# A state-space layer on one core: the cross part's products, the norm pieces and the filling rounds in another order

## The chip, the core and the metric

The kernel runs on one core of a Trainium2 chip. A core has five engines with queues of their own: TensorE (PE, matrix products), VectorE (DVE), ScalarE (ACT), GpSimd (POOL) and SyncE (SP, which here only issues DMA transfers). The metric is the device time of one execution in microseconds. The kernel before took 2694.33 us, the median of three runs (2692.2 to 2698.51).

## The reference

The whole kernel is a decoder of twelve layers on x of 32 sequences by 128 tokens by 128 channels, all in fp32. Only the first layer, a state-space layer, matters here. Its reference, cut to what matters (h counts 32 heads of 8 channels, the state has 128 entries, a chunk has 64 tokens, so that each sequence has two chunks):

```python
zxbcdt = einsum('bld,kd->blk', layernorm(x), in_proj_w)
z, xBC, dt_raw = split(zxbcdt)                  # 256, 512, 32 columns
xBC = silu(sum(xp[:, k:k + L] * conv_w[:, k] for k in range(4)) + conv_b)
x_ssm, B, C = split(xBC)                        # 256, 128, 128
dt = 0.001 + 0.099 * sigmoid(dt_raw + dt_bias)
dA = -exp(A_log) * dt;  Acum = cumsum(dA within a chunk)
L[q, s] = exp(Acum[q] - Acum[s]) for s <= q, else 0
y  = (C B^T * L) (x_ssm * dt)                   # inside a chunk
y += exp(Acum) * C (state after the chunk before)   # the cross part
y  = norm(y + D * x_ssm, gated with silu(z)) out_proj, layernorm, added to x
```

What the kernel calls the *cross part* is the contribution of the first chunk of a sequence to the second one: a product of the scaled x of the first chunk with the C B^T block across the chunks, times a decay that is spread over the heads by another product.

## The kernel before

**Work.** The 32 sequences form eight groups (G) of four (J). A *round* n works on one sequence, i = n // 4 is its group and j = n % 4 its place in the group. Rounds run from n = -2 to 31 (the loop begins at L1138). A round lasts about 9 us and a group some 37 to 40 us.

**Parts of a round.** `first(n)` (L966) runs two rounds ahead: a set of small products that this text calls *p1* (decays and C B^T blocks), their copy to the tile `cbl` on ACT (128x320, and an exponential of 64 columns), and the transposes *p2* of the convolved x, whose copy feeds the scaled tiles `right`, `xd`, `xe` on POOL. `second(n)` (L998) makes the 128x512 products into the two "two" tiles one round ahead, `exponentials` takes them on ACT (two of 128x1024), `weighted(n, 0)` and `weighted(n, 1)` multiply them with C B^T on DVE. `third(n)` (L1017) is the round's own 64 products into "acc", followed by the cross part: four products into a "ps" tile, a copy of it to `cbl` on ACT (128x256), and a multiplication on DVE that writes the tile `offs`.

**Parts of a group.** These are generators, of which `go` runs one step at a time: `entry` (L923; layer norm: statistics on DVE, a power on POOL, the four ACT activations to `xn` as its third step, the transposes to `xnT` as the fourth, and four ACT activations of the residual x as the fifth), `conv` (L862; four 128-channel blocks c = 0 to 3; for c = 2 the four taps are four products on PE, the `taps` products, for the others an ACT scaling and three multiply-adds on DVE follow the projection, then a tanh on ACT and a final multiplication on DVE), `gate` (L892; projection, copy to z, tanh on ACT, a multiplication on DVE), `decays` (L936; the product for dt, which DVE reads first into the tile `dts`, a tanh, small DVE operations, a second small product and an exponential), `joined` (L1040; sums the parts, gates, projects out, normalizes, adds to x).

**What sets the order.** PE, ACT and DVE keep the order in which the program is written: the class `Ordered` chains each instruction of an engine to the one before it, and `follow(T, A, V)` at L1097 switches that on for the layer. POOL is kept in order only in the prologue (L1098 to L1137); in the rounds a scheduler orders it. The DMA issues of SP are in program order. The PSUM tiles named "ps" have two buffers for everything (`ps()`, L220), so a product into a "ps" tile waits for the copy out of the tile two "ps" tiles earlier.

**Prologue and end.** The head of the kernel (from L284) issues the loads; `weights()` prepares the weights in two pieces; `fill()` clears and fills the kept tiles on POOL; `make_taps()` multiplies the taps of block 2 into the projection; then a list of `go` calls prepares group 0 and part of group 1 (L1100 to L1136). In the last rounds the next layer's generator `lead` (L1313) is run a step at a time: `prepare(0, 0)` loads a context tile and normalizes group 0's x (`normed`, L395, with its four scalings on POOL into `xn`), `prepare(0, 1)` transposes these on PE, then projections, and so on. In the kernel before, its steps run at the ends of rounds 27 to 31, and twice behind the loop.

Of the kernel before, what the change touches and what calls it, by code (L numbers as in the profile page):

```python
# [23 lines left out]
G = 8  # L24
J = 4
# [180 lines left out]
def program(ctx, tc, cols, x, ctxt, mask, drop, dfirst, dsmall, dwide, drows, dunits, dexperts, dconst, drel, dwq, out):  # L206
    nc = tc.nc
    V, A, T = (Ordered(tc, engine) for engine in (nc.vector, nc.scalar, nc.tensor))
    P, SY = Ordered(tc, nc.gpsimd), nc.sync
# [10 lines left out]
    def ps(shape=(128, 512), dtype=F32):  # L220
        return pp.tile(list(shape), dtype, tag="ps", name="ps", bufs=2)
# [14 lines left out]
    def gmid(shape=(128, 512), dtype=F32):  # L236
        return mid.tile(list(shape), dtype, tag="gmid", name="gmid", bufs=10)
# [41 lines left out]
    K = {n: cconst.view(cs, n) for n in cconst.at if cconst.at[n][1] < cconst.kept}  # L279
    ident = K["ident"]  # L280
# [2 lines left out]
    xg = []  # L283
    for i in range(G):  # L284
        t = const.tile([128, J, D], F32, name=f"x{i}")
        SY.dma_start(out=t, in_=x[i * J : i * J + J].rearrange("b s d -> s b d"))
        xg.append(t)
        if i == 0:
            SY.dma_start(out=ident, in_=dconst[:, 0:128])
            SY.dma_start(out=cs[:, 128:], in_=dconst[:, 128 : cconst.kept])  # L290
            w0 = units.tile([128, cfirst.n], F32, tag="unit", name="w0")
            A.dma_start(out=w0, in_=dfirst)
            ww = const.tile([128, cwide.n], F32, name="ww")
            A.dma_start(out=ww[:, 0 : cwide.early], in_=dwide[:, 0 : cwide.early].to_broadcast([128, cwide.early]))
# [6 lines left out]
    W0 = {n: cfirst.view(w0, n) for n in cfirst.at}  # L301
# [13 lines left out]
    onesb = const.tile([128, 128], BF16, name="onesb")  # L315
    V.memset(onesb, 1.0)
    identb = const.tile([128, 128], BF16, name="identb")
    V.tensor_copy(identb, ident)

    pick16 = const.tile([128, 4], BF16, name="pick16")  # L320
    V.tensor_copy(pick16, K["pick16"])
    flip = const.tile([128, 128], BF16, name="flip")
    V.tensor_copy(flip, W0["flip"])
    ctxT = [const.tile([128, 512], F32, name=f"ctxT{i}") for i in range(G)]


# [489 lines left out]
    def layer0(lead):  # L816
# [3 lines left out]
        def weights():  # L820

            A.activation(na, WW["m_A_log"], AF.Exp)
            V.tensor_scalar(na, na, -1.0, None, ALU.mult)
            yield
            for b in range(2):
                mean, block = small(1), W0["out"][:, b * 128 : b * 128 + 128]
                V.tensor_scalar(block, block, W0["norm_w"][:, b : b + 1], None, ALU.mult)
                V.tensor_reduce(mean, block, AX.X, ALU.add)
                V.tensor_scalar(mean, mean, -1.0 / 128, None, ALU.mult)
                V.tensor_scalar(block, block, mean[:, 0:1], None, ALU.add)  # L830
            V.tensor_scalar(W0["D"], W0["D"], 0.25, None, ALU.mult)
            yield

        block2 = W0["xbc"][:, 256:384]
# [2 lines left out]
        def make_taps():  # L837

            d, p = bmid((128, 4, 128)), ps((128, 4, 128))
            V.tensor_tensor(d, bc(ident, 1, 4), bc(W0["cw"][:, 8:12], 2, 128), ALU.mult)  # L840
            mm(flat(p), block2, flat(d))
            A.copy(taps[:, 0:512], flat(p))

        kept = [gbig((128, 2, 1024)) for _ in range(3)]
# [1 line left out]
        sides = [kept[0][:, n].rearrange("p (j s r c) -> p j s r c", j=J, s=2, r=4) for n in range(2)]  # L846

        def fill():
            for t in (*kept[0:2], more):
                P.memset(t, 0.0)  # L850
            for t in sides:
                for token, side, at in ((0, 0, 0), (64, 0, 8), (0, 1, 16)):
                    one = bc(bc(ident[:, token : token + 1], 1, J), 2, 4)
                    P.tensor_copy(t[:, :, side, :, at : at + 8], one.to_broadcast([128, J, 4, 8]))

        xds = [t.rearrange("p (a n m e) -> p a n m e", a=8, n=4, m=4) for t in (kept[1][:, 0], kept[1][:, 1], more[:, 0:1024])]
        rights = [kept[2][:, n, 0:512].rearrange("p (a k) -> p a k", a=8) for n in range(2)]
# [159 lines left out]
        def third(n):  # L1017

            i, j = n // J, n % J
            (xd, xe, cbl, _), m = fronts.pop(n), mids.pop(n)[0].rearrange("p s h q -> p (s h) q")  # L1020
            if j == 0:
                sums[i] = [acc((128, 2, J, 64)) for _ in range(2)]
                offs[i] = gmid((128, 2, J, 64))
            for b in range(2):
                for k in range(4):
                    for r in range(4):
                        for ch in range(2):
                            rows = slice(64 * ch, 64 * ch + 64)
                            mm(sums[i][ch][32 * r : 32 * r + 32, b, j], flat(xd[rows, 4 * b + r, k]), m[rows, 16 * b + 4 * r + k],
                               k == 0, k == 3)  # L1030
            p = ps((128, 2, 2, 64))
            for b in range(2):
                mm(p[:, 0, b], xe[:, 128 * b : 128 * b + 128], cbl[0:64, 64:128])
            for b in range(2):
                mm(p[:, 1, b], K["spread"][:, 128 * b : 128 * b + 128], cbl[:, 320:384])
            A.copy(cbl[:, 128:384], p.rearrange("p s b q -> p (s b q)"))
            both = cbl[:, 128:384].rearrange("p (s b q) -> p s b q", s=2, b=2)
            V.tensor_tensor(offs[i][:, :, j], both[:, 0], both[:, 1], ALU.mult)
# [50 lines left out]
        def go(what, g, *more):  # L1089

            if 0 <= g < G:
                key = what, g, *more
                if key not in late:
                    late[key] = what(g, *more)
                next(late[key], None)
# [6 lines left out]
        go(entry, 0)  # L1102
        go(entry, 0)
        fill()
        make_taps()
        go(entry, 0)
        next(prepared)
        go(conv, 0, 2)
        go(decays, 0)
        go(conv, 0, 3)  # L1110
        go(conv, 0, 2)
        go(entry, 1)
        go(conv, 0, 3)
        go(decays, 0)
        go(conv, 0, 2)
        go(conv, 0, 3)
        go(conv, 0, 0)
        go(decays, 0)
        go(entry, 1)
        go(conv, 0, 3)  # L1120
        go(conv, 0, 0)
        go(conv, 0, 1)
        go(decays, 0)
        go(conv, 0, 3)
        go(entry, 1)
        go(conv, 0, 0)
        go(conv, 0, 1)
        go(conv, 0, 0)
        go(conv, 0, 1)
        go(entry, 1)  # L1130
        go(conv, 0, 0)
        go(decays, 0)
        go(conv, 0, 1)
        go(conv, 0, 1)
        next(prepared)
# [2 lines left out]
        for n in range(-2, G * J):  # L1138
            i, j = n // J, n % J

            convs_now = [(1, 2)] if n == -2 else [(1, 3), (1, 0)] if n == -1 else [(i + 1, 1) if j == 0 else (i + 2, (2, 3, 0)[j - 1])]

            def go_conv():
                for g, c in convs_now:
                    go(conv, g, c)

            front = first(n + 2) if n + 2 < G * J else iter(())
            next(front, None)
            go_conv()
            next(front, None)  # L1150
            go_conv()
            if j == 0:
                go(decays, i + 1)
                go(gate, i, 0)
                go(joined, i - 2)
            elif j == 1:
                go(joined, i - 1)
            elif j == 2:
                go(decays, i + 2)
                go(decays, i + 2)  # L1160
                go(entry, i + 3)
                go(joined, i - 1)
            elif j == 3:
                go(gate, i + 1, 1)
                go(entry, i + 3)
                go(joined, i - 1)
            if 0 <= n + 1 < G * J:
                second(n + 1)
            go_conv()
            if 0 <= n + 1 < G * J:  # L1170
                exponentials(n + 1)
            if j == 1:
                go(joined, i - 1)
            elif j == 3:
                go(entry, i + 3)
            if 0 <= n + 1 < G * J:
                weighted(n + 1, 0)
            if 0 <= n < G * J:
                third(n)
            if 0 <= n + 1 < G * J:  # L1180
                weighted(n + 1, 1)
            if j == 0:
                go(entry, i + 2)
                go_conv()
            elif j == 1:
                go(entry, i + 2)
            elif j == 2:
                go(decays, i + 2)
                go(gate, i + 1, 1)
                go_conv()  # L1190
            elif j == 3:
                go(joined, i)
                go(gate, i + 1, 0)
                go_conv()
                go(decays, i + 2)
            go_conv()
            if n == -1:
                go(entry, 1)
            if n >= G * J - 5:
                next(lead)  # L1200
        next(lead)
        go(joined, G - 1)
# [1311 lines left out]
```

## Time and profile before

| | |
|---|---|
| median of three runs | 2694.33 us (2692.2 to 2698.51) |
| profiled execution | 2692.69 us, span 2690.9 us |
| mean granted clock of PE | 0.946 |
| state-space layer | 0 to about 365 us of the span |
| busy from 45 to 345 us (300 us) | PE 270.12, DVE 247.63, ACT 195.11, POOL 154.55 us |
| granted clock of PE there | 0.91 |
| busy from 0 to 45 us (prologue) | PE 26.55, DVE 22.87, ACT 18.88, POOL 14.14 us |

All times are microseconds from the start of the span. A line of the list in order of time has the start, the duration, the engine, the line of the helper that recorded it (L194 for nearly all, so that the tiles tell instructions apart), the operation, the tiles written and read with their shapes, how many instructions are merged (x4), and in brackets the idle time of the engine just before, with what ended it. A tile's buffer number is left out. A line of the waits has the engine that waited and its tile, after the arrow the engine and tile that ended the wait, then the total, the number and the longest. A line of the windows has the stretch, its length, the busy time of PE, of PE's weight loads, DVE, ACT and POOL (with their instructions), the granted clock of PE (1.00 is full speed, 0.50 half), the DMA engines' share and GB/s. The chain that ended last is told in pieces of start, duration, engine and tile.

### The profile page before, as it was taken

To read this page: it belongs to the slowest core of one execution; us is meant where nothing else is said; L and a number is where in the kernel's file an instruction comes from. 1 tells how busy PE (TensorE), PEld (TensorE's weight loads), DVE (VectorE), ACT (ScalarE), POOL (GpSimd) and SP (SyncE) were. 2 spreads that over 40 slices of the span, in tenths; PEclk is the share of its full clock that TensorE was granted. 3 is DMA by queue.
4 is the path that set the end of the run, shared out by engine and by line. 5 is a ranking of instruction groups with operands and counts; after the bars stand their busy time and mean duration, and the time that the engine had idled before them with its cause. 6 is when DMAs were issued, how large, how long until landed. Compare 5 with 4: busy or idle time off the path is not lost.

```text
span 2690.9 us, 59184 instructions
## 1 busy us (share of the span) xinstructions
PE 2387.5 (89%) x24663; PEld 1527.2 (57%) x24663; DVE 1983.8 (74%) x3972; ACT 1347.3 (50%) x2999; POOL 927.1 (34%) x979
## 2 busy tenths in 40 slices
PE   6999889999989999999998999988888987887755
PEld 3665567777744435556764444446665886544434
DVE  6888778888888756777776555569996338898993
ACT  5766544444422223344443445468983334665653
POOL 3454532322310214345651101144443444332432
PEclk8999899999999999999998999999998998998886
DMA  3000000000000010000000000000003463100000
GB/s 113 3 2 14 10 21 5 9 5 4 18 12 1 0 36 3 3 14 14 12 3 17 1 0 1 1 1 2 2 2 129 147 214 130 62 16 16 28 12 20
DMA packets 51966, 74.23 MB, mean 28 GB/s; under 512 B 4017, under 2 KB 42450, under 8 KB 51570
## 3 DMA queue, kind: packets, MB, share of 16 engines
q1 hardware_dynamic: 48786, 64.10, 7.5%
q0 software_dynamic: 2624, 5.40, 0.6%
q8 instruction: 194, 3.18, 0.5%
q10 hardware_dynamic: 288, 0.95, 0.1%
q14 instruction: 74, 0.61, 0.1%
HBM read 57.54 MB, written 12.89 MB: 26 GB/s over the span
## 4 chain that ended last, share of the span: by engine, by line
PE 56%; DVE 22%; ACT 6%; issue 2%; POOL 2%; DMA 0%; DVEq 0%; ACTq 0%; POOLq 0%
PE two L194 20%; PE ps L194 18%; PE acc L194 17%; DVE bbig L194 9%; DVE s L194 7%; ACT bbig L194 3%; DVE bmid L194 3%; POOL xn L194 1%; DVE x L194 1%; ACT bmid L194 1%; DVE gmid L194 1%; POOL s L194 1%; DVE h L194 0%; ACT L194 0%; ACT gmid L194 0%
## 5 line engine op out<-in xcount | busy, mean ns | idle before, releaser
L194 PE MATMUL two<-xnT,u 128*128 128x512 f32 x512 | 261.7, 612 | 9.3 <-ACT bmid L194 5.6
L194 DVE TENSOR_REDUCE s<-two 128x8 f32<-128x1024 f32 (+1 forms) x192 | 228.8, 1219 | 47.6 <-PE two L194 43.0
L194 DVE TENSOR_TENSOR bbig<-bbig 128x1024 f32<-128x1024 f32 (+3 forms) x232 | 248.2, 1111 | 14.3 <-ACT bbig L194 12.0
L194 PE MATMUL acc<-bmid,u 128*128 128x512 f32 x416 | 215.0, 603 | 13.4 <-DVE bmid L194 12.4
L194 PE MATMUL ps<-cs,bbig 128*128 128x128 f32 x1184 | 176.5, 289 | 47.6 <-ACT bbig L194 21.3
L194 DVE TENSOR_TENSOR bmid<-bmid,ps 128x512 f32<-128x512 f32 x192 | 129.9, 684 | 93.1 <-ACT bmid L194 71.0
L194 PEld LDWEIGHTS ps<-cs,bbig 128*128 128x128 f32 x1184 | 135.1, 146 | 101.2 <-ACT bbig L194 36.5
L194 PE MATMUL two<-gbig,gmid 32*128 32x512 f32 (+1 forms) x1248 | 186.3, 551 | 4.4 <-issue 2.1
L194 POOL TENSOR_TENSOR s<-s,nhalf 128x4 f32<-128x4 f32 x104 | 128.7, 1237 | 135.1 <-DVE s L194 116.5
L194 PEld LDWEIGHTS two<-xnT,u 128*128 128x128 f32 x512 | 91.4, 191 | 115.7 <-issue 56.6
L194 ACT ACTIVATE bbig<-two 128x1024 f32<-128x1024 f32 x96 | 94.8, 1025 | 116.7 <-PE acc L194 101.7
L194 DVE RECIPROCAL s<-acc 128x128 f32<-128x128 f32 x96 | 91.3, 951 | 83.6 <-PE acc L194 83.4
L194 ACT COPY bbig<-ps 128x512 f32<-128x512 f32 x166 | 91.4, 585 | 116.4 <-PE ps L194 116.3
L194 POOL TENSOR_TENSOR x<-x,ww 128x512 f32<-128x512 f32 x64 | 91.6, 1431 | 163.1 <-ACT xn L194 80.3
L194 ACT ACTIVATE bmid<-two,ws 128x512 f32<-128x512 f32 x128 | 85.2, 686 | 111.6 <-PE two L194 111.4
L194 POOL TENSOR_TENSOR bbig<-bbig,s 128x1024 f32<-128x1024 f32 x32 | 61.7, 1927 | 222.6 <-PE two L194 152.5
L194 ACT ACTIVATE bmid<-two 128x512 f32<-128x512 f32 x88 | 52.5, 597 | 164.0 <-PE two L194 159.2
L194 PEld LDWEIGHTS acc<-bmid,u 128*128 128x128 f32 x416 | 75.0, 192 | 101.0 <-issue 46.1
L194 ACT ACTIVATE bbig<-two,s 128x256 f32<-128x256 f32 x256 | 118.1, 477 | 25.4 <-DVE s L194 25.3
L194 ACT ACTIVATE bbig<-bbig,s 128x128 f32<-128x128 f32 x384 | 118.8, 390 | 6.8 <-DVE s L194 6.8
L194 POOL TENSOR_SCALAR gbig<-bmid,cs 128x512 f32<-128x512 f32 x64 | 99.2, 1566 | 49.0 <-ACT bmid L194 49.0
L194 PE MATMUL two<-xT,we 128*128 128x128 f32 (+1 forms) x576 | 100.4, 330 | 15.9 <-ACT xT L194 9.8
(331 smaller groups left out, 6267.0 us busy)
## 6 DMA issues: line engine op xcount, KB each, us to landing
we<-in_experts SPq DMA_DIRECT2D x36, 768.0 KB, 4.6
u<-in_units SPq DMA_DIRECT2D x10, 768.0 KB, 4.3
gmid<-in_ctx SPq DMA_DIRECT2D x16, 256.0 KB, 3.0
x<-in_x SPq DMA_DIRECT2D x8, 256.0 KB, 5.6
gmid<-in_mask SPq DMA_DIRECT2D x8, 256.0 KB, 3.1
ys<-bbig SPq DMA_DIRECT2D x2, 1024.0 KB, 6.2
gmid<-ys SPq DMA_DIRECT2D x8, 256.0 KB, 3.1
gmid<-in_drop SPq DMA_DIRECT2D x8, 256.0 KB, 3.5
```

The lines of the kernel that those rows point to most:

```text
L194: d = self.made = f(*args, **kwargs)
```

## The change

The work and the number of instructions stay the same. Seven things move:

1. the identity's load is issued ahead of the first tile of x on SP;
2. three casts on DVE (identb, pick16, flip) move from the head to the second piece of `weights()`;
3. `fill()` writes the sides right after the first memset, and clears the two other tiles behind them;
4. the cross part leaves `third(n)`, where it stood behind the round's sums and between the two weighted multiplications, and becomes `cross(n)`, called at the top of round n, ahead of `first(n + 2)`;
5. the list of `go` calls in the prologue has another order;
6. in rounds with j = 3, the step of `entry(i + 3)` with the four activations to xn moves from ahead of the weighted multiplication to behind the gate's copy and tanh;
7. the lead of the next layer runs at rounds 26, 28, 29, 30 and 31 instead of 27 to 31, so that its first step is one round earlier.

```diff
@@ the head
+        if i == 0:
+            SY.dma_start(out=ident, in_=dconst[:, 0:128])
         SY.dma_start(out=t, in_=x[i * J : i * J + J].rearrange("b s d -> s b d"))
         xg.append(t)
         if i == 0:
-            SY.dma_start(out=ident, in_=dconst[:, 0:128])
...
-    V.tensor_copy(identb, ident)
-    V.tensor_copy(pick16, K["pick16"])
-    V.tensor_copy(flip, W0["flip"])
@@ weights(), second piece
             V.tensor_scalar(W0["D"], W0["D"], 0.25, None, ALU.mult)
+            V.tensor_copy(identb, ident)
+            V.tensor_copy(pick16, K["pick16"])
+            V.tensor_copy(flip, W0["flip"])
             yield
@@ fill()
-            for t in (*kept[0:2], more):
-                P.memset(t, 0.0)
+            P.memset(kept[0], 0.0)
             for t in sides:
...
+            for t in (kept[1], more):
+                P.memset(t, 0.0)
@@ third(n)
-            (xd, xe, cbl, _), m = fronts.pop(n), mids.pop(n)[0].rearrange("p s h q -> p (s h) q")
+            xd, m = fronts.pop(n)[0], mids.pop(n)[0].rearrange("p s h q -> p (s h) q")
             if j == 0:
                 sums[i] = [acc((128, 2, J, 64)) for _ in range(2)]
-                offs[i] = gmid((128, 2, J, 64))
...
+        def cross(n):
+
+            i, j = n // J, n % J
+            _, xe, cbl, _ = fronts[n]
+            if j == 0:
+                offs[i] = gmid((128, 2, J, 64))
             p = ps((128, 2, 2, 64))
             for b in range(2):
                 mm(p[:, 0, b], xe[:, 128 * b : 128 * b + 128], cbl[0:64, 64:128])
@@ the prologue
         go(entry, 0)
         go(entry, 0)
         fill()
+        go(entry, 0)
+        go(conv, 0, 3)
+        go(decays, 0)
         make_taps()
-        go(entry, 0)
+        go(conv, 0, 3)
+        go(decays, 0)
+        go(entry, 1)
+        go(conv, 0, 3)
         next(prepared)
+        go(decays, 0)
+        go(conv, 0, 0)
         go(conv, 0, 2)
         go(decays, 0)
         go(conv, 0, 3)
+        go(conv, 0, 0)
         go(conv, 0, 2)
         go(entry, 1)
...
@@ the rounds
+            if 0 <= n:
+                cross(n)
             front = first(n + 2) if n + 2 < G * J else iter(())
...
             if j == 1:
                 go(joined, i - 1)
-            elif j == 3:
-                go(entry, i + 3)
             if 0 <= n + 1 < G * J:
                 weighted(n + 1, 0)
...
             elif j == 3:
                 go(joined, i)
                 go(gate, i + 1, 0)
+                go(entry, i + 3)
                 go_conv()
                 go(decays, i + 2)
...
-            if n >= G * J - 5:
+            if n >= G * J - 6 and n != G * J - 5:
                 next(lead)
```

More of the change, by code (lines that the diff above doesn't have):

```diff
@@ L1113, in layer0 @@
         go(conv, 0, 3)
-        go(decays, 0)
         go(conv, 0, 2)
-        go(conv, 0, 3)
+        go(conv, 0, 1)
+        go(conv, 0, 0)
+        go(entry, 1)
+        go(conv, 0, 1)
         go(conv, 0, 0)
@@ L1119, in layer0 @@
         go(entry, 1)
[L1120 to L1126, printed above, removed]
         go(conv, 0, 1)
         go(conv, 0, 0)
[L1129 to L1132, printed above, removed]
         go(conv, 0, 1)
```

## The prediction

> **What bounds the kernel now.** I read the waits of VectorE (DVE) and TensorE (PE) between 45 and 345 us of the span first, because the change touches only the state-space layer, which ends near 365 us; then the instructions in order of time around one round boundary, around the lead-in of the next layer and at the layer's end; last the busy time and granted clock of short windows.
>
> Waits of DVE, then of PE, 45 to 345 us (who waits, for whom: total us, times, longest):
>
> ```profile
> DVE bbig L194 <- ACT bbig L194: 16.3, 8, 8.0
> DVE gmid L194 <- ACT bmid L194: 11.6, 5, 5.3
> DVE dts L194 <- PE ps L194: 8.4, 6, 2.2
> DVE gmid L194 <- ACT cbl L194: 7.8, 13, 1.0
> PE ps L194 <- ACT cbl L194: 13.0, 20, 1.3
> PE ps L194 <- POOL xn L194: 6.1, 4, 3.6
> ```
>
> The reader is to see two things. DVE waits 8.4 us for the decay product (dts), six times, once in each group that still prepares a later one. So a group is a loop of two stretches: one that DVE fills, from dts to the end of convolution 1's three multiply-adds (148.03 to 173.33, 25.3 us), and a chain over PE and ScalarE (ACT) back to the next dts (136.63 to 148.03, 11.4 us). What lengthens the chain is paid each time. The row of 7.8 us is the wait that the change goes after: offs behind the cross part's copy.
>
> The chain in order of time (start, duration, engine, operation, idle before):
>
> ```profile
> 134.51 0.39 ACT L194 COPY cbl<-ps 128x256 f32<-128x256 f32 x1
> 134.76 0.62 ACT L194 COPY xnT<-ps 128x512 f32<-128x512 f32 x1
> 136.03 3.66 PE L194 MATMUL ps<-xnT,taps 128*128 128x512 f32 x8
> 136.72 0.63 ACT L194 ACTIVATE bmid<-gmid 128x512 f32<-128x512 f32 x1 [1.34 <-DVE gmid L194]
> ...
> 141.10 1.94 ACT L194 ACTIVATE bbig<-two 128x1024 f32<-128x1024 f32 x2
> ...
> 143.95 0.39 ACT L194 COPY cbl<-ps 128x256 f32<-128x256 f32 x1
> 144.20 1.67 ACT L194 ACTIVATE x<-x,s 128x128 f32<-128x128 f32 x4
> 145.75 0.43 ACT L194 COPY cbl<-ps 128x320 f32<-128x320 f32 x1
> ...
> 148.03 0.29 DVE L194 TENSOR_TENSOR dts<-ps,ww 128x128 f32<-128x128 f32 x1 [1.12 <-PE ps L194]
> ```
>
> The taps product (convolution 2) starts while ACT still waits 1.34 us for DVE with its tanh of convolution 1. The cross copy (128x256) stands ahead of that tanh at 134.51, and ahead of the residual's four activations at 143.95.
>
> **The change, part by part.** No instruction is added or removed; every cost is one of order. The sum is against the profiled execution (2692.69 us, span 2690.9), which lies 1.64 us under the median of the runs.
>
> *Cross part, j=1.* With two buffers for all "ps" tiles, each product waits for the copy out of the tile two earlier. Today the sequence is cross, xnT, p1, taps; then it is xnT, cross, p1, taps. So taps needs the cross copy, and in ACT's new order that copy stands behind the tanh that waits for DVE. New start of taps: the tanh's end, 0.39 for the copy, 0.07 to PE. At 136.72 that is 137.8 instead of 136.03, +1.77; at 98.27 it is +1.83; at 213.08, 173.53 and 252.03 it is +1.62, +0.97, +0.97, but there PE is at half clock until a fixed moment, so half of it comes back (0.81, 0.49, 0.49); at 64.99 ACT does not wait for DVE, +0.1. Sum +5.5; the bounds are 0 (all absorbed) and 7.3 (nothing comes back). Behind taps on PE stand p2, second and the exponentials' input, so DVE's weighted waits in its turn.
>
> *Cross part, j=2.* The cross copy now stands behind the four activations of x (1.67). Convolution 3's buffer is the cross's, so its product, its copy and the decay product follow in a row. From the exponentials' start: exponentials 1.81 and squares 1.04 to the next start, x 1.55, cross copy 0.43, product 1.12, bmid copy 0.66, decay product 1.19 to dts: 7.8, against 6.93 now (141.10 to 148.03). +0.87, six groups: +5.2. Bounds: 0, and 2.06 a group (all of 1.67 and 0.39), 12.4.
>
> *Offs behind the weighted pair.* The wait leaves the middle of the DVE stretch. Most of the 7.8 us becomes a wait at weighted or at dts instead, since those come from PE; in the stretch that DVE itself bounds I find 0.16 to 0.36 per group: -1.5. Bounds 0 and -7.8.
>
> *Norm pieces (xn, four activations, 1.65) behind the gate's copy and tanh, j=3.* PE gets the gate's tile back 1.65 us sooner (its waits for z are 4.4 us in all), but the next group's dts exponential, the cross copy and p1 come 1.5 to 1.85 later. I take 0: ACT has 2.5 us of wait for DVE in that round (at 131.24 it waits 2.49), which covers it; without that cover +1.85 per group, 11.1, and the best case is the z wait back, -4.4.
>
> *Clock.* Busy time in windows of the trace, ending with the clock granted:
>
> ```profile
> 134.11:137.52 3.41, 2.56 (x14) 1.72 (x15) 3.34 (x4) 2.07 (x5) 0.42 (x1) 1.00 0.00 0
> 168.24:171.65 3.41, 2.19 (x62) 1.77 (x43) 3.38 (x7) 3.41 (x7) 2.35 (x2) 1.00 0.02 5
> 171.66:178.48 6.82, 6.82 (x16) 3.83 (x17) 6.75 (x9) 1.49 (x4) 2.32 (x2) 0.50 0.00 0
> 209.20:212.61 3.41, 2.24 (x18) 1.93 (x17) 3.34 (x6) 3.09 (x5) 2.23 (x2) 1.00 0.03 5
> 212.62:216.02 3.40, 3.40 (x10) 1.70 (x9) 3.37 (x5) 1.07 (x3) 1.31 (x2) 0.50 0.00 0
> ```
>
> Second column: PE busy. After 2.56 us of 3.41 the clock stays at 1.00, after 2.19 and 2.24 the next window is granted 0.50, and taps takes 6.10 (173.53) instead of 3.66. The change takes 1.8 us out of the 2.56 of the first window. I charge the two groups at full clock now (98 and 136) about 2 us each: +4, nearer to the throttled rows than to none. Bounds 0, and six times 2.44 = 14.6.
>
> The Trainium skill ("TensorE: Matmul & The Clock Gate", "What's actually happening" and "HAM oscillation — how this bites in real kernels") says that the array falls to half rate after an idle window of about 3.4 us and comes back after a busy one. The longest idle time of PE ahead of 171.66 is 1.03 us, so the trace throttles earlier than the rule as worded. By the rule this term is 0 and the sum below 4 us lower; the rows decide.
>
> *Lead of the next layer one round earlier.* PE waits for POOL's norm with all its later work queued behind (PE is kept in order), then ACT and DVE:
>
> ```profile
> 323.59 6.06 POOL L194 TENSOR_SCALAR xn<-x,s 128x128 f32<-128x128 f32 x4
> 325.74 0.48 PE L194 MATMUL ps<-cs,xn 128*128 128x128 f32 x1 [3.57 <-POOL xn L194]
> 328.15 0.48 PE L194 MATMUL ps<-cs,xn 128*128 128x128 f32 x1 [1.94 <-POOL xn L194]
> 335.57 1.23 DVE L194 SCALAR_TENSOR_TENSOR bbig<-bbig,cbl 128x1024 f32<-128x1024 f32 x1 [7.97 <-ACT bbig L194]
> ```
>
> With xn ready, the transposes end near 322.8, and p1 (1.06), p2, second and the first exponential follow at their full-clock rows: weighted near 328.1 instead of 335.57, -7.4. The context load (256 KB, 3.0 us) on SP's queue moves with it; nothing of this layer stands behind it on that queue, so no cost. On POOL the norm (0.58, 1.25, 6.06) passes ahead of right(29), which makes second(29) about 1.8 late on PE; DVE is behind there, so I charge 0.4. Sum -7.0; bounds -9 (the half clock at 325 to 335 goes too) and +1.8 (right(29)'s delay paid in full, no gain).
>
> *End of the layer.*
>
> ```profile
> 353.71 2.10 PE ps L194 x8
> 355.90 0.38 ACT cbl L194
> 356.31 2.53 DVE gmid L194 x7
> ```
>
> This is the chain that ended last: the cross part lies between the last sum and the join. At the top of the round it is out of the way: 2.6 from 353.71 to 356.31. What is late next is the 16 "two" products (3.79) that stand behind it on PE and only move by 2.1, into DVE's reduces: I take -1.6, bounds -2.6 and 0.
>
> *Prologue.* The identity ahead of x0 on SP and two casts (0.23, 0.22) out of DVE's head remove its wait of 1.51; xnT (15.25) comes about 2.3 us earlier, and the cold taps product (6.42) no longer stands ahead of the decays (DVE idles 6.92 there). But taps must run later on the same PE, the weights' second part ends near 40 us in both, and x0's four loads land behind one more transfer: -1.0, bounds -3 and +0.5. Fill's other order and the casts lie beside idle time (POOL, 8.57 us of wait). Offs in rounds 26 to 30 outside the lead: -0.4 (waits of 0.63, 0.64, 0.73, mostly passed on); bounds -2 and 0.
>
> Sum: 5.5 + 5.2 - 1.5 + 4.0 - 7.0 - 1.6 - 1.0 - 0.4 = +3.2, so 2695.9 against the profiled execution and 2697.5 against the median; I say 2698. 0.2% is 5.4 us, about what a measurement of this kernel can tell from no change.
>
> **Rivals.**
> A (the sum): 2698, its own range 2692 to 2705.
> B, the clock decides: every group loses one taps pass to half clock. Six times 2.44 instead of 4.0 is +10.6: 2708. For it: windows at 2.56 busy lose 0.9 to 1.8. Against: the groups at 173, 213 and 252 us are throttled already, and a taps pass that is at half clock cannot lose the same 2.44 again.
> C, faster: the delays of j=1 and j=2 do not reach dts, because DVE arrives there later than the product. Then 5.5, 5.2 and 4.0 fall away, and 2698 - 14.7 = 2683. It decides if DVE comes over 1.1 to 1.3 us later to dts relative to PE than now (its waits at 110.26 to 266.47); the weighted pair, which moves with the exponentials, could do that. Against it: those waits exist in all six groups, so DVE is early today.
> D, the lead does not gain: POOL is late with right(29) and PE waits for that instead of xn. +7.0: 2705.
>
> **How the numbers follow.** Chances: A 0.46, B 0.22, C 0.24, D 0.08. A lies mostly within 0.2% (2688.9 to 2699.7): of it 0.27 same, 0.16 slower, 0.03 faster. B and D are slower, C faster. So faster 0.27, same 0.27, slower 0.46. The range 2684 to 2711 leaves out the better half of C and the worse third of B; A's neighbours and the bounds of the clock term fill the rest.
>
> **What would show it.** Right: the taps rows at 136.03 and 98.27 start about 1.1 us after convolution 1's last multiply-add ends; the cross copy stands behind the tanh; the wait of dts for PE grows from 8.4 to some 20 us; the offs wait vanishes from the DVE list; the 7.97 wait and the four waits for xn are gone; the join follows the last sum directly. Wrong: if dts waits no longer than now (C), if PE's mean clock from 45 to 345 us falls well below 0.91 (B), or if second(29) waits for POOL by over 3 us (D). Most likely to fail are the two chain terms, since they assume that nothing else shifts beside them.

## The result, and the profile after

The changed kernel takes 2714.74 us, the median of seven runs (2706.46 to 2723.93), against 2695.59 us for the kernel before on the same chips (seven runs, 2691.57 to 2698.51): a ratio of 1.0075, 95% interval 1.0057 to 1.0093. It is slower by 20 us, not by 4: outside the stated range of 2684 to 2711, on the side of rival B.

The profiled execution took 2716.11 us with a span of 2714.3 us. Three marks place the loss inside the layer: the first and the last dts row of the rounds on VectorE (DVE), and the first instruction of the join that ends the layer.

| | before | after | difference |
|---|---|---|---|
| first dts of the rounds | 42.0 | 41.0 | -1.0 |
| last dts (six groups later) | 266.5 | 288.4 | |
| the six groups between them | 224.5 | 247.4 | +22.9 |
| from the last dts to the join | 90.1 | 86.2 | -3.9 |
| join | 356.5 | 374.6 | +18.0 |
| from the join to the end of the execution | 2336.2 | 2341.6 | +5.4 |

The last row is scatter: the work behind the join is the same, and it took 2334 to 2346 us in the executions profiled here. So the six groups lose 23 us and the tail gains 4. The 1.0 us at the first dts says nothing yet: in the two other profiles with the prologue of before (the runs with the lead alone, below) the first dts came at 39.2 and 42.1, in those with the changed prologue between 39.9 and 42.1.

The stretch from 45 to 345 us, by busy time in the views of windows, here of after (columns: length, busy PE, PE's weight loads, DVE, ACT, POOL, then PE's granted clock):

```profile
45.00:345.00 300.00, 269.29 (x4727) 177.97 (x4726) 233.43 (x440) 184.87 (x363) 134.37 (x143) 0.84 0.02 6
```

Before, the clock there was 0.91 and PE was busy 270.12 us over 5220 matmul records; now it is busy as long for 4727 records. Since the clock is granted at 1.00 or 0.50 in all these traces, a mean of 0.91 is some 54 us at half clock in these 300 us (2 x 0.09 x 300), and 0.84 some 96 us.

The waits of DVE, PE and ScalarE (ACT) there, of after:

```profile
DVE dts L194 <- PE ps L194: 14.5, 5, 3.5
...
DVE gmid L194 <- ACT cbl L194: 6.4, 6, 1.2
...
PE ps L194 <- ACT cbl L194: 11.1, 7, 3.7
PE ps L194 <- ACT dts L194: 10.0, 6, 2.1
...
ACT bmid L194 <- DVE gmid L194: 5.3, 3, 2.5
```

DVE waits for dts 14.5 us instead of 8.4. The wait for offs has not gone: it is 6 waits, 6.4 us in all, instead of 13 and 7.8. New is the row in which PE waits for ACT's dts, 10.0 us (1.2 before). And ACT's wait for DVE ahead of its tanh and its copies is down to 5.3 us; the same row of before reads

```profile
ACT bmid L194 <- DVE gmid L194: 21.1, 11, 2.6
```

In the list in order of time, of after, one group shows two waits of PE:

```profile
129.95 1.64 ACT L194 ACTIVATE xn<-x,s 128x128 f32<-128x128 f32 x4
...
132.01 0.25 ACT L194 ACTIVATE dts<-ps 64x128 f32<-64x128 f32 x1
132.17 0.35 ACT L194 COPY cbl<-ps 128x256 f32<-128x256 f32 x1
...
132.31 0.71 PE L194 MATMUL ps<-w,gbig 128*128 128x64 f32 x4 [1.57 <-ACT dts L194]
...
141.43 3.66 PE L194 MATMUL ps<-xnT,taps 128*128 128x512 f32 x8
...
149.34 1.65 ACT L194 ACTIVATE x<-x,s 128x128 f32<-128x128 f32 x4
...
150.88 0.69 ACT L194 COPY cbl<-ps 128x256 f32<-128x256 f32 x2
...
151.30 1.13 PE L194 MATMUL ps<-xnT,w 128*128 128x512 f32 x2 [1.40 <-ACT cbl L194]
```

(The copy x2 at 150.88 is the cross copy and the 128x320 copy behind it, merged.) At j=3 the four xn activations now stand ahead of the decays' exponential, and p1, at the top of the next round, waits 1.57 us for it. At j=2 the cross copy stands behind the x activations, and convolution 3 waits 1.40 us. Each returns five times in the layer, at 1.57 to 1.58 and at 1.40 us. What follows two of them is in the windows, of after:

```profile
105.75:109.15 3.40, 2.00 (x19) 1.73 (x18) 2.15 (x3) 3.40 (x9) 1.89 (x2) 1.00 0.00 0
109.17:115.98 6.81, 6.56 (x24) 5.02 (x25) 3.30 (x13) 2.13 (x6) 4.12 (x6) 0.50 0.02 4
129.64:133.04 3.40, 1.83 (x14) 1.62 (x14) 3.40 (x7) 2.88 (x8) 0.00 (x0) 1.00 0.01 2
133.06:136.46 3.40, 3.40 (x14) 1.74 (x16) 3.37 (x11) 1.35 (x5) 2.22 (x1) 0.50 0.00 0
```

The wait of 1.40 us leaves a window with 2.00 us of work, the wait of 1.57 one with 1.83; the clock then is 0.50 for 6.81 and 3.40 us. Of the ten waits, nine have half clock that begins between 1.1 us before and 2.3 us after their end; behind the one that ends at 242.92 the clock stays at 1.00. How full the window is, is a sign and not a rule: from 45 to 345 us of this trace, 11 of the 13 full-clock windows of 3.41 us ahead of half clock held 0.00 to 2.48 us of PE work, the other two 2.90 and 3.08, while the 46 followed by another at full clock held 2.32 us or more.

### The profile page after: what moved, and what is told of

Read it like the earlier page. It is cut to its first block, busy times and chain, and to the rows that moved or that the text cites. A ratio compares the mean times of both kernels' runs of the same rounds, so it can differ in the third digit from the quotient of the medians.

```text
span 2714.3 us, 59212 instructions
## 1 busy us (share of the span) xinstructions
PE 2411.2 (89%) x24644; PEld 1544.4 (57%) x24663; DVE 1986.5 (73%) x3972; ACT 1349.1 (50%) x2999; POOL 920.1 (34%) x979
## 4 chain that ended last, share of the span: by engine, by line
PE 64%; DVE 22%; ACT 8%; issue 3%; POOL 2%; DMA 1%; SPq 0%; ACTq 0%; DVEq 0%; POOLq 0%
PE ps L194 25%; PE two L194 21%; PE acc L194 18%; DVE bbig L194 9%; DVE s L194 7%; ACT bbig L194 4%; DVE bmid L194 3%; ACT bmid L194 2%; POOL xn L194 1%; DVE x L194 1%; DVE gmid L194 1%; ACT xn L194 1%; POOL s L194 1%; ACT gmid L194 0%; ACT L194 0%
## 5 line engine op out<-in xcount | busy, mean ns | idle before, releaser
L194 PE MATMUL acc<-bmid,u 128*128 128x512 f32 x416 | 213.9, 601 | 13.8 <-DVE bmid L194 12.4
L194 POOL TENSOR_TENSOR bbig<-bbig,s 128x1024 f32<-128x1024 f32 x32 | 61.7, 1927 | 224.5 <-PE two L194 151.8
```

The lines of the kernel that those rows point to most:

```text
L194: d = self.made = f(*args, **kwargs)
```

## The experiments

The runs come from several chips, so times below are given as ratios to the kernel before as it ran beside each of them; differences of ratios are turned into microseconds of 2694 us.

### Which part costs: the moves put back

Two theories. *Gaps*: the two waits of PE throttle its clock, so both moves cost. *Ledger*: the recorded sum, in which the cross part carries all cost and the norm pieces none.

The norm pieces alone put back:

```diff
+            elif j == 3:
+                go(entry, i + 3)
             if 0 <= n + 1 < G * J:
                 weighted(n + 1, 0)
...
                 go(gate, i + 1, 0)
-                go(entry, i + 3)
                 go_conv()
```

> The changed kernel with only the four xn activations put back ahead of the weighted multiplication (j=3). Gap theory (two new PE waits per group, p1 on the decay exponential behind xn, 1.57 us, and convolution 3 on the cross copy behind the x activations, 1.40 us, each answered by windows at half clock): p1's 1.57 wait is gone, the stretch from the first to the last decay product of the rounds falls from 247 us to about 236, run about 2703 us. Ledger theory (the prediction's sum: the norm pieces cost 0, the cross part's two chain terms cost all): 2714 us as in the changed kernel.

> The version with only the xn activations put back, again, as the upper end for the filled wait: 2708 us on both theories.

The cross part alone put back (`cross(n)` called behind the sums of `third(n)` again), and both put back:

```diff
-            if 0 <= n:
-                cross(n)
             front = first(n + 2) if n + 2 < G * J else iter(())
...
                 third(n)
+                cross(n)
```

> The changed kernel with only the cross part put back behind the round's sums. Gap theory: the 1.40 wait is gone and p1's 1.57 wait stays, stretch about 236 us, run about 2702 us. Ledger theory: everything that costs is gone, stretch 224 to 226 us, run about 2688 us (lead and prologue keep their gain, the end of the layer loses 1.6).

> The changed kernel with the cross part and the xn activations both put back: what is left is the earlier lead, the prologue and the first loads. Both theories: stretch 224 us as before the change; the lead's gain of 7 us and the prologue's 1 us show alone, run about 2687 us. If the lead's gain was never there, 2694 us.

> The version with both parts put back once more, beside the candidate and with more rounds: 2679 us, ratio 0.996 to the kernel before, on every theory; it settles how much of the lead's and prologue's gain is more than scatter.

| | ratio (95%) | median us | six groups, us | clock 45 to 345 |
|---|---|---|---|---|
| the change | 1.0075 (1.0057 to 1.0093) | 2714.74 | 247.4 | 0.84 |
| xn put back | 1.006 (1.0037 to 1.0084) | 2708.6 | 243.7 | 0.84 |
| again | 1.0052 (1.0033 to 1.0071) | 2710.25 | 250.7 | 0.81 |
| cross put back | 0.9992 (0.9974 to 1.0009) | 2688.83 | 230.0 | 0.89 |
| both put back | 0.9961 (0.9946 to 0.9976) | 2679.22 | 218.4 | 0.93 |
| again | 0.9957 (0.9942 to 0.9972) | 2680.72 | 218.4 | 0.93 |

Both theories miss a part. With the norm pieces still moved and the cross part back, the run costs 0.0031 to 0.0035, 8 to 9 us, more than with both back: there the ledger's 0 is refuted (2683 to 2696 us in ten executions against 2677 to 2688 in ten beside them). Against the change the same move is worth 0.0015 to 0.0023, 4 to 6 us, but those two intervals overlap, and of the two profiles one has shorter and one longer groups than the change (243.7 and 250.7 against 247.4), so in that pairing it is not separated. With both back the kernel is faster than before by 11 us. The cross part is the greater cost, 22 us between the change and the run with it put back (0.0083), and that is more than twice the ledger's 10.7 for its two chain terms. The steps close: 11 us gained with both back, 8 to 9 lost by the norm pieces, 22 by the cross part, make the 20 of the change.

### The wait at j=2, and what is left without it

The x activations go behind the cross copy (the step of `entry` moves from the end of round j=1 to the top of round j=2). In the first of these runs the xn activations are put back, in the second they stand behind the decays' exponential:

```diff
             if j == 0:
                 go(entry, i + 2)
                 go_conv()
-            elif j == 1:
-                go(entry, i + 2)
...
                 cross(n)
+            if n >= 0 and j == 2:
+                go(entry, i + 2)
             front = first(n + 2) if n + 2 < G * J else iter(())
```

> The changed kernel with the xn activations put back and, besides, the x activations behind the cross copy; the cross part stays at the top. Against the run with only xn put back (2708.6 us) it shows the price of the 1.40 us wait at j=2. If that wait and the windows after it are the greater part of the cross part's cost: 2690 us. If the cost lies in the j=1 place (tanh of convolution 1 ahead of the copy): 2703 us or more.

> The version with the xn activations put back and the x activations behind the cross copy, again, as the lower end for the filled wait: 2686 us on both theories.

> The changed kernel, cross part still at the top of the round, with the xn activations moved one step further, behind the decay exponential, and the x activations moved behind the cross copy of the next round. Gap theory: both waits of PE are gone though the cross part stays where the change put it; clock from 45 to 345 us back to about 0.91, run 2685 to 2690 us. Ledger theory: the term of j=1 (5.5 us, the tanh of convolution 1 ahead of the cross copy) stays, run about 2697 us. If the place of the cross part itself throttles PE: 2705 us or more.

With xn put back and x behind the copy: 0.997 (0.9954 to 0.9985) and 0.9973 (0.9962 to 0.9985), 2686.64 and 2686.11 us. Against the runs with only xn put back that is 0.0079 to 0.0090, 21 to 24 us, for one step of ACT. In order of time, of this run, the second time:

```profile
145.96 0.39 ACT L194 COPY cbl<-ps 128x256 f32<-128x256 f32 x1
146.21 1.67 ACT L194 ACTIVATE x<-x,s 128x128 f32<-128x128 f32 x4
...
146.45 1.12 PE L194 MATMUL ps<-xnT,w 128*128 128x512 f32 x2
...
147.76 0.43 ACT L194 COPY cbl<-ps 128x320 f32<-128x320 f32 x1
```

The copy is out of the way when convolution 3 needs the buffer, and its wait is gone. The order of j=1 is still the changed one. What remains against the kernel with both back is 0.0009 to 0.0016, 2 to 4 us, with overlapping intervals; in the profiles the join comes 6 to 8 us later. That is the cross part at the top with j=1's and offs' terms in it, priced at 5.5 - 1.5 = 4.0. But the wait that this price stands for, of taps for the cross copy, hardly occurs: of the twelve taps passes in the groups of these two runs four wait, by 0.39 to 0.61 us, 2.2 us in all. What has grown is PE's wait for the gate's z copy, which now holds up the cross products: 11.0 us from 45 to 345 us, against 5.1 with both put back.

With xn behind the exponential instead: 1.0 (0.9985 to 1.0016), 2691.03 us, which is 0.0027 to 0.0030, some 8 us, behind the version with xn in its old place. It missed the 2685 to 2690 expected of the gap theory, by 1 us: p1 no longer waits 1.57 us each time, the clock is back at 0.91 as expected, and yet xn late on ACT costs. PE waits 15.7 us there for copies to cbl, 9.1 with xn in its old place, but 4.5 instead of 11.0 for z; which of these waits costs the 8 us was not tried.

### Is it the clock? PE kept busy in its waits

Products that nobody needs are added. They write into the round's own "two" tile, which the real products overwrite.

```diff
+        def warm(n):
+            warmed[n] = [two((128, 2, 8, 64)) for _ in range(2)]
+            mm(flat(warmed[n][0][:, 0]), ident, W0["xbc"][:, 0:512])
...
                 cross(n)
+            if 0 <= n < 26 and j == 0:
+                warm(n + 1)
             front = first(n + 2) if n + 2 < G * J else iter(())
             next(front, None)
+            if 0 <= n < 26 and j == 2:
+                warm(n + 1)
             go_conv()
```

> The changed kernel plus work that nobody needs: one fp32 product of 128x512 (1.08 us at full clock) into the round's own two tile, which its real products overwrite, at the two places where PE waits in each group: behind the cross part at j=0 and ahead of convolution 3 at j=2 (13 products in all, 14 us of PE at full clock). Clock theory (the half-clock windows are what costs, and they are caused by these two idle places): mean clock from 45 to 345 us rises from 0.84 to 0.89 or more, the stretch between the decay products falls from 247 to 235 us, run 2700 us or less in spite of the added work. Chain theory (the waits cost by their own length, the clock is a by-product): the added products lengthen PE's queue or change nothing, run 2714 us or more.

The control has the same 13 products behind the cross part at j=1 and j=3 instead (`if 0 <= n < 26 and j in (1, 3)`):

> The control for the run with added products: the changed kernel with the same 13 products of 128x512 that nobody needs, but behind the cross part at j=1 and j=3, where PE does not wait. If the gain of the added products came from filling the two idle places, it is not there now: both waits of 1.57 and 1.40 us stay, clock from 45 to 345 us at 0.86 or less, run 2714 to 2728 us. If any more work on PE lifts the clock, wherever it stands, 2700 us again.

In the waits: 1.0016 (0.9999 to 1.0033), 2698.44 us; 16 us less than the change, with some 14 us of work added. Elsewhere: 1.0039 (1.0022 to 1.0057), 2707.44 us. The view of windows, first of the run with the products in the waits, then of the control:

```profile
45.00:345.00 300.00, 269.49 (x5099) 174.73 (x5098) 252.96 (x460) 193.62 (x382) 156.61 (x158) 0.94 0.02 7
```

```profile
45.00:345.00 300.00, 268.31 (x4943) 176.39 (x4942) 242.16 (x454) 190.31 (x376) 142.37 (x153) 0.92 0.02 7
```

The control did not do what was expected of it: the clock rose to 0.92 there too, although both waits of PE stayed, as its waits show:

```profile
PE ps L194 <- ACT dts L194: 10.0, 6, 2.1
PE ps L194 <- ACT cbl L194: 9.9, 9, 1.4
```

So added work lifted the clock at both pairs of places, and a good clock alone does not give all the time back: the control gained some 10 us on the change, the run with the waits filled 16; their six groups took 244.4 (in an execution of 2713.2 us, the longest of its five) and 236.1 us against 247.4. In the control the products stand in the queue's way, in the waits they lie beside ACT's work. This pair does not say what share the clock has, which is why the j=2 wait was taken alone: xn put back, the wait left as it is, one product inside it.

> The changed kernel with the xn activations put back and, in each j=2 round, one product of 128x512 that nobody needs (1.08 us) inside PE's wait of 1.40 us ahead of convolution 3: the wait stays, the idle time goes. If the half clock is the greater part of the wait's price: near the version without the wait, 2692 us or less. If the wait's own length is the greater part: near the version with the wait not filled, 2704 us or more. In between, the two parts can be read off.

```profile
148.20 1.65 ACT L194 ACTIVATE x<-x,s 128x128 f32<-128x128 f32 x4
...
148.69 1.12 PE L194 MATMUL two<-w,cs 128*128 128x512 f32 x2
...
149.74 0.69 ACT L194 COPY cbl<-ps 128x256 f32<-128x256 f32 x2
...
150.16 1.12 PE L194 MATMUL ps<-xnT,w 128*128 128x512 f32 x2 [0.34 <-ACT cbl L194]
```

Convolution 3 still starts behind the copy, but PE's idle time ahead of it is 0.34 us. The run takes 1.0005 (0.9993 to 1.0018), 2696.93 us, beside 2710.25 with the wait not filled and 2686.11 without the wait, all on one chip. Of the 24.1 us, 13.3 go when only the idle time is filled, and the mean clock from 45 to 345 us rises from 0.81 to 0.90: the best reading is that this part is half clock. Whether the six products would have gained as much elsewhere, as 13 of them partly did in the control, was not tried in this version. The other 10.8 stay, 1.8 us in each of six groups: the wait's own length on the chain, and whatever the added product costs.

### The gains: lead, prologue, and two candidates

The early lead alone in the kernel before (only the condition on n), and the head with the filling rounds alone in the kernel before:

> The kernel before with only the lead of the next layer one round earlier. The kernel with lead, prologue and first loads was 13 us faster than before. Theory 1 (the lead gives what PE's wait for the norm cost, 7 us, and the prologue little): 2685 us. Theory 2 (the prologue's other phase against the clock's windows gives the larger part): 2689 to 2692 us, and the stretch of the groups stays at 224 us.

> The kernel before with the early lead alone, again, with more rounds. If the profile's reading holds (the tail of the layer from the last decay product to the join 6.7 us shorter): 0.9975, some 2687 us. If the first measurement's middle holds: 0.9992, some 2692 us.

> The kernel before with only the head and the filling rounds of the change (loads, casts, fill, the list of steps). The lead alone gave 0.9992 of the time, lead and prologue together 0.9961. If the two add: 0.997, about 2686 us, though the first decay product of the rounds comes only about 1 us earlier; the gain then lies in another position against the clock's windows in the groups. If they do not add (the difference is scatter): 0.9996, about 2693 us.

The lead alone: 0.9992 (0.9977 to 1.0007) and 0.9988 (0.9972 to 1.0003), 2 to 3 us, which both intervals allow to be nothing. PE's waits for xn are gone in it, and the tail from the last dts to the join is 83.4 and 83.2 us instead of 90.1, as priced; in the two profiled executions that is 7 us, in the medians less than half. That gap stays open. DVE's waits in order of time show where a part went. Before, besides the one of 7.97 us at 335.57:

```profile
306.76 1.23 DVE L194 SCALAR_TENSOR_TENSOR bbig<-bbig,cbl 128x1024 f32<-128x1024 f32 x1 [5.66 <-ACT bbig L194]
...
356.31 0.29 DVE L194 TENSOR_TENSOR gmid<-cbl 128x128 f32<-128x128 f32 x1 [4.70 <-ACT cbl L194]
```

The lead alone, the second time:

```profile
304.00 1.23 DVE L194 SCALAR_TENSOR_TENSOR bbig<-bbig,cbl 128x1024 f32<-128x1024 f32 x1 [5.23 <-ACT bbig L194]
...
319.83 2.73 DVE L194 SCALAR_TENSOR_TENSOR bmid<-bmid,s,ww 128x128 f32<-128x128 f32 x4 [2.18 <-POOL s L194]
...
347.17 0.29 DVE L194 TENSOR_TENSOR gmid<-cbl 128x128 f32<-128x128 f32 x1 [3.02 <-ACT cbl L194]
```

The wait of 7.97 us is gone; the one of 5.2 us was there before. New are 2.2 us for POOL, which now has the norm of the next layer ahead of this layer's power.

The head and the filling rounds alone: 0.9975 (0.9963 to 0.9988), 2687.92 us, 7 us where 1 was priced. In its profile the first dts is 1.5 us earlier (40.5), but the six groups take 218.1 us instead of 224.5, with the same instructions in the same order on PE, ACT and DVE. What differs is the clock (windows over the six groups, first before, then this run):

```profile
42.00:266.50 224.50, 206.00 (x3756) 133.22 (x3756) 196.09 (x374) 156.61 (x316) 112.06 (x116) 0.92 0.02 6
```

```profile
40.50:258.50 218.00, 199.82 (x3756) 130.12 (x3756) 196.49 (x373) 156.52 (x316) 115.68 (x115) 0.95 0.02 6
```

Part of this is scatter: with the lead alone, which changes nothing before the last dts, the six groups took 222.2 and 222.1 us at 0.93. The version with both parts put back, with the changed prologue, took 218.4 both times at 0.95, so some 4 us are left for the prologue. Why the same groups are throttled less behind it was not tried.

Two candidates were built on the version with both parts put back. In the first only the multiplication of offs moves behind the second weighted one, and the last round has the whole cross part at its top:

> A candidate: the early lead and the prologue kept, the xn activations put back, the cross part's products and copy where the kernel before has them, only its multiplication on DVE (offs) behind the second weighted multiplication; in the last round alone the whole cross part at the top. Against the kernel with both parts put back (2679.2 us): if the waits of offs (7.8 us before, 13 times) held DVE where DVE sets the pace, 2675 us; if they only lay ahead of other waits, 2678 us from the end of the layer alone; a loss would mean that a later offs holds something back.

0.9966 (0.995 to 0.9982), 2686.77 us: no gain over 0.9961 and 0.9957, although DVE's wait of offs for ACT from 45 to 345 us falls from 6.4 us to 1.9 in it: other waits of DVE are longer there (for ACT's bmid 11.6 us where the version with both parts put back has 5.5, for the power on POOL 3.6 where it has 2.2). The second fills PE's idle time in the prologue (one product) and at the top of round 0 (two):

> A candidate: the version with both parts put back (lead and prologue kept), plus three products that nobody needs: one in PE's idle time ahead of group 1's transposes in the prologue, two at the top of round 0, where PE waits 3.48 us for the gate's copy. Clock theory: the half-clock stretches near 31 to 38 and 52 to 65 us shrink or go, the group behind them gains its wait of 5 us at 70 us, 2674 us against 2679. If the early groups are bound by ACT and DVE: 2679 us; more if the products are in the way.

0.9952 (0.9933 to 0.9971), 2679.0 us, beside 0.9957. The clock is 1.00 from 0 to 80 us, where the version without the products has, in its first profile, 0.92 to 45 us and 0.80 behind it. The second dts comes 5.3 us earlier for it (71.40 instead of 76.74), but the last dts and the join come at the same time (260.3 and 260.1, 342.2 in both). The groups between lose the lead again, at a lower clock; the view of windows from the second to the last dts, first without the products, then with them:

```profile
76.74:260.05 183.31, 169.35 (x3378) 111.62 (x3378) 174.63 (x330) 131.51 (x264) 98.95 (x100) 0.97 0.02 7
```

```profile
71.40:260.29 188.89, 174.32 (x3378) 113.59 (x3378) 168.82 (x331) 131.24 (x264) 97.25 (x100) 0.95 0.02 7
```

So PE's clock does count in the first of these groups, and what is won there is lost again in the groups behind, where more of the time is at half clock. The version with both parts put back, with or without these products, beats both kernels.

## Why the prediction was wrong, step by step

- **Clock, +4.0.** The kind of cost was right, place and size were not. The step took the throttle from the j=1 window of the two groups that were at full clock, and its price was a taps pass at half clock; taps started at 141.43 in the quoted group, 1.0 us after convolution 1's last multiply-add, as foretold, but PE had no wait of 0.5 us or more there, and all six taps passes ran at full clock (3.66 us each; before, four of the six took 4.07 to 6.11). The throttle came at the two other waits instead, nine times out of ten. At j=2 alone some 13 us go with the filled idle time.
- **Cross part, j=2, +5.2.** The chain was read correctly (copy behind x, then convolution 3, then dts), the size was not: 10.8 us stay with the idle time filled, near the upper bound of 12.4, and 13.3 go with it. The term counted how far the chain's steps overlap at full clock, and took PE's wait for free in the meantime.
- **Norm pieces, 0.** This step failed by its cover. It said that ACT's 2.5 us of wait for DVE at 131.24 hide the delay of the exponential. But on ACT that wait stands behind the exponential, and PE waits for the exponential first; in order of time, of before:

```profile
128.04 0.25 ACT L194 ACTIVATE dts<-ps 64x128 f32<-64x128 f32 x1
...
128.35 1.13 PE L194 MATMUL ps<-xnT,w 128*128 128x512 f32 x2 [0.20 <-ACT dts L194]
...
131.24 0.59 ACT L194 COPY bmid<-ps 128x512 f32<-128x512 f32 x1 [2.49 <-DVE gmid L194]
```

With the norm pieces alone moved (the run with the cross part put back):

```profile
130.98 1.63 ACT L194 ACTIVATE xn<-x,s 128x128 f32<-128x128 f32 x4
...
133.04 0.25 ACT L194 ACTIVATE dts<-ps 64x128 f32<-64x128 f32 x1
...
133.34 2.07 PE L194 MATMUL ps<-xnT,w 128*128 128x512 f32 x2 [0.92 <-ACT dts L194]
```

There PE's waits for the exponential are 9.5 us in all, 1.2 before, although the cross part is in its old place. Measured 8 to 9 us (4 to 6, not separated, in the changed kernel); the bound stated without the cover was 11.1.
- **Cross part, j=1, +5.5, and offs, -1.5.** Together 4.0, measured 2 to 4, not clear of nothing, with what the top of the round does to the layer's end in it. The size is near, but by luck: the wait of taps that the term was made of hardly occurs, and PE waits for z instead. That the offs wait would vanish was wrong: 6.4 us of it stand in other places, and where it was nearly removed, nothing was gained.
- **Lead, -7.0.** The waits for xn and DVE's 7.97 us are gone, as foretold, and in the profiles the tail shrinks by 6.6 to 6.8 with the lead alone; in the medians it is 2 to 3, not clear of 0. In the changed kernel the tail shrinks by 3.9 only, to 86.2, at a mean clock of 0.85. The place of the cross part is not the reason: the two runs with x behind the copy have it at the top too and the same program behind the last dts, and their tails are 80.8 and 81.4, at 0.94.
- **End of the layer, -1.6.** The join does follow the last sum directly: the sum ends at 374.53 and the join starts at 374.56, where 2.8 us lay between them before. From the end of the last weighted multiplication to the join it is 4.3 us, and 5.1 with both put back, both at full clock, so the order is worth 0.8 there, half of the price.
- **Prologue, -1.0.** The first dts is 1.0 to 1.5 us earlier, which is no more than the scatter of that mark with an unchanged prologue (39.2 to 42.1); of the 7 us measured some 4 come with a better clock in the groups behind it, and for the rest no row accounts.

The terms that separate 3.2 from 20 are j=2, at 24 instead of 5.2 with the clock behind its wait in it, and the norm at 4 to 9 instead of 0; lead and prologue gained 11 together instead of 8. The rival that described the outcome, B, had 0.22 of the chance and named the clock, but with the taps pass as the place. Its case against, that three groups were throttled already, was mistaken: those throttles were at j=1, the new ones came at other places, and half clock grew by some 42 us.

The Trainium skill's rule ("TensorE: Matmul & The Clock Gate", "HAM oscillation — how this bites in real kernels") would have put the clock term at 0, since no wait of PE in the six groups is near 3.4 us; waits of 1.40 and 1.57 us were enough in these traces, as in the two windows above with 2.00 and 1.83 us of work. The same page, in its section on a second failure mode ("psum-queue depth-cycling"), says that frequent short idle times of PE between groups of matmuls, as buffers in PSUM are cycled, can make the clock oscillate, there in a bf16 kernel; the filled wait, 13 us, agrees with that.

## What to carry to other kernels

Moving work later on an in-order engine is paid where the next user of its buffer stands: ask of each copy out of PSUM what is put ahead of it, and who waits for that buffer. A wait of PE that would cost its own 1.4 us can cost as much again through the clock, so look at the busy time that is left in the window around it and not at the wait alone. And one engine's wait for another covers a delay only for the instructions behind that wait: here the exponential that PE needed stood 3 us ahead of it.

## What was not expected of the hardware

The 13 added products raised the granted clock also where they stood in the way (0.84 to 0.92), but the time followed in full only where PE had been idle: 2707 against 2698 us, from 2715. Without one instruction of theirs changed, six groups took 218 us behind one prologue and 222 to 224 behind the other (clock 0.95, and 0.92 to 0.93). And with the clock at 1.00 for the first 80 us, the first group was 5.3 us earlier and the layer ended at the same microsecond, since half clock came back in the groups behind it.
